# Neighbour sums by one float32 product in place of two float32r terms

## The chip, the cores and the metric

The kernel runs on one core of a Trainium2 chip. The metric is the device time of one execution in microseconds (us); lower is better. The engines are named as in the profile: PE is TensorE (matmuls), PEld its weight loads, DVE is VectorE, ACT is ScalarE, POOL is GpSimd and SP is SyncE, which only issues DMAs here.

## The reference

There are 4096 nodes with 512 features each, an adjacency matrix of 4096 x 4096 integers of 0 or 1 (a share of 0.0078 ones), and two layers.

```python
# layer 0
Ab = adj > 0
keep = Ab & (cumsum(Ab, axis=1) <= 64)            # the first 64 neighbours of each row
cnt = keep.sum(axis=1, keepdims=True)
nb_mean = (keep @ x) / maximum(cnt, 1.0)
xj = leaky_relu(nb_mean @ W_nb.T + b_nb)
xi = leaky_relu(x @ W_line.T + b_line)
x = layernorm(x + xi + where(cnt > 0, xj, 0))
# layer 1
Wh = x @ W + bW
e = (Wh @ a1 + b1)[:, None] + (Wh @ a2 + b2)[None, :]
e = where(e > 0, e, 0.2 * e)
e = where(adj > 0, e, -9e15)
x = layernorm(x + softmax(e, axis=1) @ Wh)
```

## The kernel before

The rows are cut into NB = 32 blocks of P = 128. The order of instructions on each engine is written by hand (`tc.manual_schedule()`): each engine executes its own in program order. Layer 0 computes y = x @ W_nb.T first, and then the neighbour sums keep @ y, which is the same as (keep @ x) @ W_nb.T.

**The maps.** A loop over g = 1 to NT - 1 = 15 (and a last call that finishes) calls `seven(g, last, codes)` for a pair of blocks. It computes x @ W_nb.T and x @ W_line.T for both with seven half products in place of eight, by sums and differences of operands (Winograd's form of Strassen's scheme). A product is two matmuls of 512 float32 columns (L512). PE adds into PSUM banks `bank_x`, `bank_y`, `bank_z` and `bank_w`; ACT copies between banks (L568, L578, L579), and DVE adds (L576, L594), forms the sums of x (L503 to L508) and transposes x in squares of 32 (L297). `y_terms` takes each block of y out of PSUM: ACT writes `y_hi`, y rounded to float32r (L427), and DVE writes `y_lo` = y - `y_hi` (L428). Blocks 26 to 29 have no room yet: they are kept whole and written to `y_d` in DRAM (L426); `room_again` takes back rooms that the maps used and loads these four blocks, and at step 2 of the sums they are split in two (L730, L731).

**The chunks of flags.** Between the steps of a round the kernel works on the adjacency matrix in chunks of 128 rows by CH = 2048 columns, two for each block, 64 in all. For one chunk: `load_adj` loads 1 MB by SP's queue into one of two buffers; `edge` (L171, ACT) makes flags of it; `scan_sums` (L189 to L194, DVE) counts along the row; `scan_codes` (L201 and L202, DVE) writes what remains after the limit of 64; `pack` (L219, ACT) makes bytes of it, and POOL's queue writes them to `code_d` in DRAM (L222). A variable `done` counts chunks. Rounds 3 to 15 take one chunk each, 13 in all; the other 51 lie in the next stage.

**The neighbour sums.** A loop over s = 0 to 127: block i = s // 4, and within it group g = s % 4 of KB = 8 tiles. `load_kt` loads the bytes of a block back with a transposing DMA, two blocks ahead; `make_kt` (L274, ACT) turns them into a tile of flags `kt` of 8 x 128 x 128, two steps ahead. PE then runs, for each of the 8 tiles j, one matmul against `y_hi` and one against `y_lo`, each with the flags as the stationary operand and 512 columns:

```python
for term in (y_hi, y_lo):
    nc.tensor.matmul(
        accs[i], kt[:, k // 2, k % 2, :], term[j],
```

This line is L757 in the profile. DVE and ACT finish the block before (bias, leaky ReLU, the block's own part, layer norm; `finish`), and `codes_step` spreads the remaining chunks at 58/32 of a chunk for each block.

**Layer 1** follows (L1221 and L908: Wh, again with seven products in place of eight; L1094: attention times Wh, four steps q in each of 16 pairs of blocks, 28 matmuls of 256 columns in each step). All its matmuls are float32.

Of the kernel before, what the change touches and what calls it, by code (L numbers as in the profile page):

```python
# [9 lines left out]
F32 = mybir.dt.float32  # L10
F32R = mybir.dt.float32r
# [4 lines left out]
ALU = mybir.AluOpType  # L16
# [4 lines left out]
P = 128  # L21
# [11 lines left out]
def two_layer_adj_gnn(  # L33
# [16 lines left out]
    nc = tc.nc  # L50
    N, C = x.shape
    NB = N // P
    NC = C // P
    NT = NB // 2
    CH = 2048
    NCH = N // CH
# [40 lines left out]
    own_d = [dram.tile([P, C], F32, name=f"own_d{b}") for b in range(NB)]  # L97
    y_d = dram.tile([P, 4, C], F32, name="y_d")

# [38 lines left out]
    with ExitStack() as l0:  # L138
        adj_p = l0.enter_context(tc.tile_pool(name="l0_adj", bufs=2))
        big = l0.enter_context(tc.tile_pool(name="l0_big", bufs=1))  # L140

        last = l0.enter_context(tc.tile_pool(name="l0_last", bufs=1, reuse_waits="tile"))
        ROOM = 6
        EDGE = NB - ROOM
        y_most = [big.tile([P, EDGE, C], F32R, name=name) for name in ("y_hi", "y_lo")]
        y_hi, y_lo = ({i: t[:, i, :] for i in range(EDGE)} for t in y_most)
        ident = big.tile([P, P], F32, name="ident")
# [6 lines left out]
        def load_adj(s, behind=None):  # L154
            if s < NB * NCH:
                b, h = divmod(s, NCH)
                a = adj_p.tile([P, CH], I32, name="a")
                if behind is not None:
                    behind.memset(a[:, 0:1].bitcast(F32), 0.0)
                nc.sync.dma_start(a, adj_blk(b)[:, ts(h, CH)])  # L160
                loaded[s] = a
# [103 lines left out]
        ktbs, kts, accs, owns, fin = {}, {}, {}, {}, {}  # L265
        y_again = []

        def make_kt(s):
            if s < NB * NS:
                b, g = divmod(s, NS)  # L270
                if s not in kts:
                    kts[s] = ktb_p.tile([P, KB // 2, 2, P], F32R, name="kt")
                bytes_ = ktbs[b].bitcast(U8)[:, ts(g, KB // 2), :]
                nc.scalar.activation(  # L274
                    kts[s], bytes_.rearrange("p t (i r) -> p t r i", r=2),
                    AF.Sigmoid, bias=steep[:, 1:2], scale=STEEP,
                )


        with ExitStack() as la:  # L280
            work = la.enter_context(tc.tile_pool(name="l0_work", bufs=2))
            wp = la.enter_context(tc.tile_pool(name="l0_w", bufs=1))

            AHEAD = 14
            bias_line = wp.tile([P, C], F32, name="bias_line")
            w_t = {}
            xrs, xbs, xts, pys, pls = {}, {}, {}, {}, {}
            lines, held = {}, []

# [105 lines left out]
            def fold_end():  # L395
                nc.vector.tensor_tensor(ca, ca, b12, ALU.add)
                nc.sync.dma_start(wa_d.rearrange("k (c p) -> p k c", p=P), wa)
# [20 lines left out]

            def y_terms(i, src):

                if EDGE <= i < NB - 2:
                    if not held:
                        held.extend((work.tile([P, C], F32, name="xb", bufs=1), room_lo[:, 5]))
                    t = held[i % 2]
                    nc.scalar.copy(t, src)
                    return lambda: nc.gpsimd.dma_start(y_d[:, i - EDGE, :], t)  # L426
                nc.scalar.copy(y_hi[i], src)  # L427
                return lambda: nc.vector.tensor_tensor(  # L428
                    y_lo[i], src, y_hi[i].bitcast(F32), ALU.subtract
                )  # L430

# [38 lines left out]

            room_hi = last.tile([P, ROOM, C], F32, name="hi")
            room_lo = last.tile([P, ROOM, C], F32, name="lo")

            def halves(t):
                return t.rearrange("p (k c) -> p k c", c=P)

            t1, t2, t4 = (room_hi[:, 2 * k : 2 * k + 2, :] for k in range(3))
            s1, s2, s4 = (
                halves(room_lo[:, k // 2, ts(k % 2, C // 2)]) for k in range(3)
            )  # L480
            w11, w21 = w_t["nb"][:, 0:2, :], w_t["nb"][:, 2:4, :]
# [5 lines left out]
            for k in range(2):  # L487
                x_low[2 * k] = halves(room_lo[:, 2 + k])

# [26 lines left out]

            y_low = [y_terms(i, pys[i]) for i in range(2)]
            turn_pair(1, 0)
# [11 lines left out]
            nc.scalar.copy(bank_z, bias_line)  # L530
            y_low[0]()
            tt(a21, a11, a21, ALU.subtract)
# [3 lines left out]
            bend(1)  # L536
            y_low[1]()
            tt(t4, w21, t2, ALU.subtract)
# [12 lines left out]
            line_tiles = [work.tile([P, C], F32, name="t", bufs=4) for _ in range(4)]  # L551
            line_tiles.append(room_lo[:, 4])

            def seven(g, last, codes):
# [9 lines left out]
                if old and new:  # L564
                    y_terms(2 * p, bank_y)()
                if new:
# [33 lines left out]
                if old and new:  # L600
                    y_terms(2 * p + 1, x_p)()
                if last:
                    room_again()
                    y_terms(2 * p, bank_y)()
                    y_terms(2 * p + 1, x_p)()
                if new:
# [11 lines left out]
            def make_first_kt():  # L618
                spare = adj_p.tile([P, CH], BF16, name="edge")
                kts[0] = spare.bitcast(F32R).rearrange("p (t r i) -> p t r i", r=2, i=P)  # L620

            def room_again():
                for y, name in ((y_hi, "hi"), (y_lo, "lo")):
                    t = last.tile([P, ROOM, C], F32R, name=name)
                    y_again.append(t[:, 0:4, :])
                    y.update((EDGE + n, t[:, n, :]) for n in range(ROOM))
                nc.sync.dma_start(y_again[1].bitcast(F32), y_d)

            idle = [lambda: None] * 4
            for g in range(1, NT):  # L630
                steps = idle
                q = done[0]
                if g == 1:
                    steps = [
                        lambda: None,
                        lambda: None,
                        lambda: nc.scalar.activation(few[:, 5:6], three, AF.Sigmoid),
                        lambda: fold_w(0),
                    ]
                elif g == 2:  # L640
                    steps = [
                        lambda: (fold_w(1), load_adj(0, nc.vector)),
                        lambda: fold_w(2),
                        lambda: None,
                        lambda: (fold_w(3), load_adj(1, nc.vector)),
                    ]
                else:
                    flags = lambda: (load_adj(q + 2), edge(q + 1))
                    codes = (lambda: pack(q - 1)) if g > 3 else (
                        lambda: (edge(0), fold_w(NC), fold_end())  # L650
                    )

                    steps = [
                        flags if g > 4 else codes,
                        lambda: scan_sums(q),
                        codes if g > 4 else flags,
                        lambda: scan_codes(q),
                    ]
                    if g == NT - 1:
                        load_own_x(NB - 1, nc.gpsimd)  # L660
                        scan_first = steps[1]
                        steps[1] = lambda: (scan_first(), load_first_kt())
                    done[0] += 1
                seven(g, False, steps)
# [6 lines left out]
        ktb_p = l0.enter_context(tc.tile_pool(name="l0_ktb", bufs=3, reuse_waits="tile"))  # L671
        RATE = 58 / 32
        start = done[0]

        def load_kt(b):
# [49 lines left out]
        for s in range(NB * NS):  # L725
            i, g = divmod(s, NS)
            if s == 2:
                for n in range(0, 4, 2):
                    hi, lo = (t[:, n : n + 2, :] for t in y_again)
                    nc.scalar.copy(hi, lo.bitcast(F32))  # L730
                    nc.vector.tensor_tensor(lo, lo.bitcast(F32), hi.bitcast(F32), ALU.subtract)  # L731
            make_kt(s + 2)
# [17 lines left out]
            kt = kts.pop(s)  # L750
            turns = list(range(KB))
            if s == NS - 1:
                turns = turns[:2] + turns[6:] + turns[2:6]
            for n, k in enumerate(turns):
                j = g * KB + k
                for term in (y_hi, y_lo):
                    nc.tensor.matmul(  # L757
                        accs[i], kt[:, k // 2, k % 2, :], term[j],
                        start=(g == n == 0 and term is y_hi),
                        stop=(g == NS - 1 and n == KB - 1 and term is y_lo),  # L760
                    )
            if g == 0:
                finish(i - 2, 4)
            finish(i - 1, g)
            codes_step(start + int((s + 1) * RATE / NS))
        finish(NB - 2, 4)
# [585 lines left out]
```

## Time and profile before

| | |
|---|---|
| time, median of 3 runs | 1550.87 us (1549.61 to 1551.31) |
| the profiled execution | 1549.75 us, its span 1548.0 us |
| granted TensorE clock | 0.999 |
| PE busy | 1537.9 us, 99% |
| DVE busy | 1265.5 us, 82% |
| ACT busy | 985.5 us, 64% |
| POOL busy | 269.5 us, 17% |
| HBM | 142.08 MB read, 43.13 MB written |

Times in the profile are microseconds unless marked ns. A busy time is the union of an engine's instructions; a matmul's record lasts until its last result is out, so records of consecutive matmuls overlap, and the time from the start of one to that of the next (its stride) is shorter than the record. The chain is the work that ended last, followed back from the last instruction.

### The profile page before, as it was taken

To read this page: it belongs to the slowest core of one execution; us is meant where nothing else is said; L and a number is where in the kernel's file an instruction comes from. 1 tells how busy PE (TensorE), PEld (TensorE's weight loads), DVE (VectorE), ACT (ScalarE), POOL (GpSimd) and SP (SyncE) were. 2 spreads that over 40 slices of the span, in tenths; PEclk is the share of its full clock that TensorE was granted. 3 is DMA by queue.
4 is the path that set the end of the run, shared out by engine and by line. 5 is a ranking of instruction groups with operands and counts; after the bars stand their busy time and mean duration, and the time that the engine had idled before them with its cause. 6 is when DMAs were issued, how large, how long until landed. Compare 5 with 4: busy or idle time off the path is not lost.

```text
span 1548.0 us, 19196 instructions
## 1 busy us (share of the span) xinstructions
PE 1537.9 (99%) x6592; PEld 1241.4 (80%) x6592; DVE 1265.5 (82%) x2349; ACT 985.5 (64%) x1190; POOL 269.5 (17%) x428
## 2 busy tenths in 40 slices
PE   9999999999999999999999999999999999999998
PEld 5444478888888888878888888888888888888887
DVE  6888759999999999378887888888888888888864
ACT  3666678888888887427685567555675556755520
POOL 4445322212222212120001101111011110111101
PEclk9999999999999999999999999999999999999999
DMA  7965598879888887653122212222122221222201
GB/s 196 249 208 185 192 251 265 251 244 256 259 257 256 238 263 193 152 135 104 47 58 55 51 32 69 66 58 51 32 69 67 57 52 33 68 67 57 52 4 55
DMA packets 178434, 203.28 MB, mean 131 GB/s; under 512 B 102224, under 2 KB 138832, under 8 KB 170016
## 3 DMA queue, kind: packets, MB, share of 16 engines
q1 hardware_dynamic: 150080, 131.78, 30.2%
q0 software_dynamic: 26544, 68.69, 16.9%
q10 hardware_dynamic: 1712, 1.59, 0.4%
q8 instruction: 52, 0.85, 0.2%
q14 instruction: 46, 0.38, 0.1%
HBM read 142.08 MB, written 43.13 MB: 120 GB/s over the span
## 4 chain that ended last, share of the span: by engine, by line
PE 98%; DMA 1%; DVE 1%; ACT 0%; ACTq 0%; issue 0%; POOLq 0%; DVEq 0%; SPq 0%
PE acc L1094 36%; PE acc L757 28%; PE pt L1094 14%; PE acc L512 11%; PE acc L908 5%; PE pt L757 2%; PE acc L1221 1%; DMA bias_line<-in_L_gnn_b_line_dram 0%; DMA a<-in_L_gnn_W_nb_dram 0%; DMA c<-in_x_dram 0%; PE acc L373 0%; PE acc L350 0%; DVE t L406 0%; DVE hi L519 0%; DVE hi L534 0%; ACTq L292 0%
## 5 line engine op out<-in xcount | busy, mean ns | idle before, releaser
L1094 PE MATMUL acc<-bt,s 128*128 128x256 f32 x1504 | 335.7, 379 | 0.0
L1094 PEld LDWEIGHTS acc<-bt,s 128*128 128x128 f32 x1504 | 285.8, 190 | 38.9
L757 PE MATMUL acc<-y_hi,kt 128*128 128x512 f32 x780 | 303.4, 389 | 0.0
L757 PE MATMUL acc<-y_lo,kt 128*128 128x512 f32 x780 | 303.4, 389 | 0.0
L979 ACT ACTIVATE w<-nat,few 128x1024 f32<-128x1024 uint8 x128 | 137.0, 1137 | 237.8 <-DVE a L1054 237.8
L1094 PE MATMUL acc<-bt,a 128*128 128x256 f32 x1056 | 239.0, 379 | 0.0
L1094 PE MATMUL pt<-bt,a 128*128 128x256 f32 x992 | 224.5, 379 | 0.0
L1094 PEld LDWEIGHTS acc<-bt,a 128*128 128x128 f32 x1056 | 200.6, 190 | 27.3
L1094 PEld LDWEIGHTS pt<-bt,a 128*128 128x128 f32 x992 | 188.5, 190 | 25.6
L1054 DVE STREAM_TRANSPOSE a<-w 128x1024 f32<-128x1024 f32 x128 | 153.2, 1226 | 61.5 <-ACT w L1035 51.0
L274 ACT ACTIVATE kt<-ktb,few 128x1024 fp32r<-128x1024 uint8 x124 | 142.7, 1152 | 87.4 <-PE acc L757 71.7
L127 POOL TENSOR_TENSOR rs<-ve,few 128x1 f32<-128x1 f32 x64 | 46.8, 731 | 811.0 <-DVE ve L125 791.1
L757 PEld LDWEIGHTS acc<-y_lo,kt 128*128 128x128 f32 x780 | 146.5, 188 | 30.5
L757 PEld LDWEIGHTS acc<-y_hi,kt 128*128 128x128 f32 x780 | 146.3, 188 | 30.4
L972 ACT ACTIVATE w<-w,st_n 128x1024 f32<-128x1024 f32 x128 | 149.3, 1233 | 16.1 <-DVE m L989 16.1
L1035 ACT ACTIVATE w<-w,nm 128x1024 f32<-128x1024 f32 x128 | 145.5, 1138 | 11.1 <-DVE nm L1026 11.1
L989 DVE CUSTOM_DVE_ANT_0 w<-e_n,w 128x1024 f32<-128x1024 f32 x128 | 149.5, 1221 | 1.3
L171 ACT ACTIVATE edge<-a,few 128x2048 bf16<-128x2048 int32 x64 | 136.3, 2130 | 6.0 <-DMA a<-in_adj_dram 6.0
L219 ACT CAST code<-left 128x2048 uint8<-128x2048 bf16 x64 | 121.1, 1892 | 0.0
L202 DVE TENSOR_TENSOR left<-edge,left 128x2048 bf16<-128x2048 bf16 x64 | 78.4, 1225 | 2.2
L190 DVE TENSOR_TENSOR_SCAN left<-few,ends,left 128x1024 bf16<-128x1024 f32 x32 | 75.2, 2351 | 1.1
L512 PE MATMUL acc<-hi,lo 128*128 128x512 f32 x160 | 73.8, 593 | 0.4 <-ACT acc L568 0.4
(236 smaller groups left out, 2048.6 us busy)
## 6 DMA issues: line engine op xcount, KB each, us to landing
a<-in_adj_dram SPq DMA_DIRECT2D x64, 1024.0 KB, 5.7
code_d<-code POOLq DMA_DIRECT2D x64, 256.0 KB, 3.8
nat<-code_d SPq DMA_DIRECT2D x248, 64.0 KB, 2.2
w<-x_d SPq DMA_DIRECT2D x128, 64.0 KB, 2.2
own<-in_x_dram SPq DMA_DIRECT2D x31, 256.0 KB, 3.1
own<-own_d POOLq DMA_DIRECT2D x31, 256.0 KB, 4.6
x_d<-own POOLq DMA_DIRECT2D x31, 256.0 KB, 4.4
out_dram<-c POOLq DMA_DIRECT2D x30, 256.0 KB, 2.8
```

Source lines behind the costliest of these rows:

```text
L171: nc.scalar.activation(edge_of[s], loaded.pop(s).rearrange("p (t q) -> p q t", q=2), AF.Sigmoid, bias=steep[:, 0:1], scale=STEEP, accum_ou ...
L202: nc.vector.tensor_tensor(left, e, left, ALU.mult)
L219: nc.scalar.copy(code.bitcast(U8).rearrange("p (t q) -> p q t", q=2), seen_of.pop(s))
L274: nc.scalar.activation(kts[s], bytes_.rearrange("p t (i r) -> p t r i", r=2), AF.Sigmoid, bias=steep[:, 1:2], scale=STEEP,)
L512: nc.tensor.matmul(bank, lhs[:, k, :], rhs[:, k, :], start=start and k == 0, stop=k == 1, skip_group_check=True,)
L757: nc.tensor.matmul(accs[i], kt[:, k // 2, k % 2, :], term[j], start=(g == n == 0 and term is y_hi), stop=(g == NS - 1 and n == KB - 1 and ...
L972: nc.scalar.activation(dst, src, AF.Prelu, bias=bias, scale=scale, alpha=0.2)
L979: nc.scalar.activation(wts[b][:, i, :], nats[b, i // 2].bitcast(U8)[:, i % 2, :], AF.Relu, bias=far, scale=-FAR,)
L989: nc.vector.tensor_tensor_reduce(w_i, e2_n, w_i, 1.0, -3e38, ALU.subtract, ALU.max, m4s[b][:, i : i + 1])
L1035: nc.scalar.activation(w_i, w_i, AF.Exp, bias=nms[b][:, i : i + 1], accum_out=z4s[g][:, r, i : i + 1])
L1054: nc.vector.transpose(a[:, r].rearrange("p s (i a) -> p i s a", a=SQ), wts[2 * g + r][:, :, ts(k, 8 * SQ)].rearrange("p i (s x) -> p i s x ...
L1094: nc.tensor.matmul(banks[g][n], lhs[:, j, :], bt[:, 4 * k + j, rhs, :], start=(k == 0 and j == 0 and n == mate[0]), stop=(k == NP - 1 and ...
```

## The change

y is kept whole, in float32: `y_all` holds all 32 blocks, `keep_y` is one copy by ACT, and the subtraction, the spill to `y_d`, `room_again` and the late splitting go. `kt` is float32, and each tile of flags is multiplied once by y (L734 of the changed kernel). The rooms of the maps become tiles of a pool of their own, `room_p`. Three more chunks of flags are placed in the maps, 16 in place of 13: the pairs of rounds 6 and 7, 9 and 10, 12 and 13 take three chunks each. The remaining 48 are spread evenly over 116 of the 128 steps of the sums.

```diff
-        y_most = [big.tile([P, EDGE, C], F32R, name=name) for name in ("y_hi", "y_lo")]
-        y_hi, y_lo = ({i: t[:, i, :] for i in range(EDGE)} for t in y_most)
+        y_all = big.tile([P, NB, C], F32, name="y")
...
-                    kts[s] = ktb_p.tile([P, KB // 2, 2, P], F32R, name="kt")
+                    kts[s] = ktb_p.tile([P, KB // 2, 2, P], F32, name="kt")
...
-            def y_terms(i, src):
-
-                if EDGE <= i < NB - 2:
-                    if not held:
-                        held.extend((work.tile([P, C], F32, name="xb", bufs=1), room_lo[:, 5]))
-                    t = held[i % 2]
-                    nc.scalar.copy(t, src)
-                    return lambda: nc.gpsimd.dma_start(y_d[:, i - EDGE, :], t)
-                nc.scalar.copy(y_hi[i], src)
-                return lambda: nc.vector.tensor_tensor(
-                    y_lo[i], src, y_hi[i].bitcast(F32), ALU.subtract
-                )
+            def keep_y(i, src):
+                nc.scalar.copy(y_all[:, i, :], src)
...
-                    flags = lambda: (load_adj(q + 2), edge(q + 1))
-                    codes = (lambda: pack(q - 1)) if g > 3 else (
-                        lambda: (edge(0), fold_w(NC), fold_end())
-                    )
-
-                    steps = [
-                        flags if g > 4 else codes,
-                        lambda: scan_sums(q),
-                        codes if g > 4 else flags,
-                        lambda: scan_codes(q),
-                    ]
+                    half = {6: 0, 7: 1, 9: 0, 10: 1, 12: 0, 13: 1}.get(g)
...
+                    elif half == 1:
+                        steps = [
+                            lambda: (pack(q - 1), scan_codes(q)),
+                            lambda: scan_sums(q + 1),
+                            lambda: flags(q + 1),
+                            lambda: (pack(q), scan_codes(q + 1)),
+                        ]
+                        done[0] += 1
+                    else:
+                        steps = [
+                            lambda: flags(q),
+                            lambda: scan_sums(q),
+                            lambda: pack(q - 1),
+                            lambda: scan_codes(q),
+                        ]
+                        if half == 0:
+                            steps[3] = lambda: (scan_codes(q), flags(q + 1), scan_sums(q + 1))
...
-            if s == 2:
-                for n in range(0, 4, 2):
-                    hi, lo = (t[:, n : n + 2, :] for t in y_again)
-                    nc.scalar.copy(hi, lo.bitcast(F32))
-                    nc.vector.tensor_tensor(lo, lo.bitcast(F32), hi.bitcast(F32), ALU.subtract)
...
-            for n, k in enumerate(turns):
+            for k in range(KB):
                 j = g * KB + k
-                for term in (y_hi, y_lo):
-                    nc.tensor.matmul(
-                        accs[i], kt[:, k // 2, k % 2, :], term[j],
-                        start=(g == n == 0 and term is y_hi),
-                        stop=(g == NS - 1 and n == KB - 1 and term is y_lo),
-                    )
+                nc.tensor.matmul(
+                    accs[i], kt[:, k // 2, k % 2, :], y_all[:, j, :],
+                    start=(j == 0), stop=(j == NB - 1),
+                )
...
-            codes_step(start + int((s + 1) * RATE / NS))
+            codes_step(start + (s + 1) * AFTER // (NS * (NB - 3)))
```

More of the change, by code (lines that the diff above doesn't have):

```diff
@@ L97, in two_layer_adj_gnn @@
     own_d = [dram.tile([P, C], F32, name=f"own_d{b}") for b in range(NB)]
-    y_d = dram.tile([P, 4, C], F32, name="y_d")
     x1_d = [dram.tile([N // 4, C], F32, name=f"x1_d{k}") for k in range(4)]
@@ L140, in two_layer_adj_gnn @@
         big = l0.enter_context(tc.tile_pool(name="l0_big", bufs=1))
-        last = l0.enter_context(tc.tile_pool(name="l0_last", bufs=1, reuse_waits="tile"))
-        ROOM = 6
-        EDGE = NB - ROOM
-        y_most = [big.tile([P, EDGE, C], F32R, name=name) for name in ("y_hi", "y_lo")]
-        y_hi, y_lo = ({i: t[:, i, :] for i in range(EDGE)} for t in y_most)
+        y_all = big.tile([P, NB, C], F32, name="y")
         ident = big.tile([P, P], F32, name="ident")
@@ L265, in two_layer_adj_gnn @@
         ktbs, kts, accs, owns, fin = {}, {}, {}, {}, {}
-        y_again = []
         def make_kt(s):
@@ L282, in two_layer_adj_gnn @@
             wp = la.enter_context(tc.tile_pool(name="l0_w", bufs=1))
+            room_p = la.enter_context(tc.tile_pool(name="l0_room", bufs=1))
             AHEAD = 14
@@ L287, in two_layer_adj_gnn @@
             xrs, xbs, xts, pys, pls = {}, {}, {}, {}, {}
-            lines, held = {}, []
+            lines = {}
             def load_squares(dst, src, queues):
@@ L465, in two_layer_adj_gnn @@
             wide = [pls[0]]
[L471 to L479, printed above, removed]
-            )
+            t1, t2, t4 = (room_p.tile([P, 2, C], F32, name=f"t{k}") for k in (1, 2, 4))
+            s1, s2, s4 = (room_p.tile([P, 2, P], F32, name=f"s{k}") for k in (1, 2, 4))
             w11, w21 = w_t["nb"][:, 0:2, :], w_t["nb"][:, 2:4, :]
@@ L487, in two_layer_adj_gnn @@
             for k in range(2):
-                x_low[2 * k] = halves(room_lo[:, 2 + k])
+                x_low[2 * k] = room_p.tile([P, NC, P], F32, name=f"x_low{k}")
             def top(g):
@@ L515, in product @@
                     )
-            y_low = [y_terms(i, pys[i]) for i in range(2)]
+            for i in range(2):
+                keep_y(i, pys[i])
             turn_pair(1, 0)
@@ L530, in two_layer_adj_gnn @@
             nc.scalar.copy(bank_z, bias_line)
-            y_low[0]()
             tt(a21, a11, a21, ALU.subtract)
@@ L536, in two_layer_adj_gnn @@
             bend(1)
-            y_low[1]()
             tt(t4, w21, t2, ALU.subtract)
@@ L551, in two_layer_adj_gnn @@
             line_tiles = [work.tile([P, C], F32, name="t", bufs=4) for _ in range(4)]
-            line_tiles.append(room_lo[:, 4])
+            line_tiles.append(room_p.tile([P, C], F32, name="line"))
             def seven(g, last, codes):
@@ L564, in seven @@
                 if old and new:
-                    y_terms(2 * p, bank_y)()
+                    keep_y(2 * p, bank_y)
                 if new:
@@ L600, in seven @@
                 if old and new:
-                    y_terms(2 * p + 1, x_p)()
+                    keep_y(2 * p + 1, x_p)
                 if last:
-                    room_again()
-                    y_terms(2 * p, bank_y)()
-                    y_terms(2 * p + 1, x_p)()
+                    keep_y(2 * p, bank_y)
+                    keep_y(2 * p + 1, x_p)
                 if new:
@@ L619, in make_first_kt, with flags @@
                 spare = adj_p.tile([P, CH], BF16, name="edge")
[L620 to L627, printed above, removed]
+                kts[0] = spare.bitcast(F32).rearrange("p (t r i) -> p t r i", r=2, i=P)
+            def flags(q):
+                load_adj(q + 2)
+                edge(q + 1)
             idle = [lambda: None] * 4
@@ L647, in two_layer_adj_gnn @@
                 else:
-                    flags = lambda: (load_adj(q + 2), edge(q + 1))
-                    codes = (lambda: pack(q - 1)) if g > 3 else (
-                        lambda: (edge(0), fold_w(NC), fold_end())
-                    )
-                    steps = [
-                        flags if g > 4 else codes,
-                        lambda: scan_sums(q),
-                        codes if g > 4 else flags,
-                        lambda: scan_codes(q),
-                    ]
+                    half = {6: 0, 7: 1, 9: 0, 10: 1, 12: 0, 13: 1}.get(g)
+                    if g < 5:
+                        codes = (lambda: pack(q - 1)) if g > 3 else (
+                            lambda: (edge(0), fold_w(NC), fold_end())
+                        )
+                        steps = [
+                            codes, lambda: scan_sums(q), lambda: flags(q), lambda: scan_codes(q)
+                        ]
[8 more added lines that the diff above has]
+                    else:
+                        steps = [
+                            lambda: flags(q),
+                            lambda: scan_sums(q),
+                            lambda: pack(q - 1),
+                            lambda: scan_codes(q),
+                        ]
+                        if half == 0:
+                            steps[3] = lambda: (scan_codes(q), flags(q + 1), scan_sums(q + 1))
                     if g == NT - 1:
@@ L671, in two_layer_adj_gnn @@
         ktb_p = l0.enter_context(tc.tile_pool(name="l0_ktb", bufs=3, reuse_waits="tile"))
-        RATE = 58 / 32
         start = done[0]
+        AFTER = NB * NCH + 1 - start
         def load_kt(b):
@@ L750, in two_layer_adj_gnn @@
             kt = kts.pop(s)
-            turns = list(range(KB))
-            if s == NS - 1:
-                turns = turns[:2] + turns[6:] + turns[2:6]
-            for n, k in enumerate(turns):
+            for k in range(KB):
                 j = g * KB + k
-                for term in (y_hi, y_lo):
-                    nc.tensor.matmul(
-                        accs[i], kt[:, k // 2, k % 2, :], term[j],
-                        start=(g == n == 0 and term is y_hi),
-                        stop=(g == NS - 1 and n == KB - 1 and term is y_lo),
-                    )
+                nc.tensor.matmul(
+                    accs[i], kt[:, k // 2, k % 2, :], y_all[:, j, :],
+                    start=(j == 0), stop=(j == NB - 1),
+                )
             if g == 0:
```

## The prediction

> **What bounds the kernel now.** I read the page first: which engine is busy, and what the chain that ended last is made of.
>
> ```profile
> span 1548.0 us, 19196 instructions
> PE 1537.9 (99%) x6592; PEld 1241.4 (80%) x6592; DVE 1265.5 (82%) x2349; ACT 985.5 (64%) x1190; POOL 269.5 (17%) x428
> PE 98%; DMA 1%; DVE 1%; ACT 0%; ACTq 0%; issue 0%; POOLq 0%; DVEq 0%; SPq 0%
> ```
>
> TensorE (PE) is busy and carries 98% of the chain, so time comes from what is put on or taken off PE; work on the others is hidden until it makes PE wait. Next, the chain in order of time (start, us, what), which says how long each PE stage lasts.
>
> ```profile
> 26.76 177.09 PE acc L512 x412
> 203.85 29.31 PE pt L757 x128
> 233.16 435.20 PE acc L757 x1920
> 668.36 10.30 PE acc L1221 x24
> ```
>
> L512 are the maps, L757 the neighbour sums, L1221 the start of layer 1. They abut: maps end at 203.85, and the sums run from there to 668.36 without a gap, 464.51 us in 2048 records. Then the two lines themselves (count, duration in ns as minimum/median/maximum, first and last start).
>
> ```profile
> L757 PE MATMUL acc<-y_hi,kt x780: 389/389/389, 233.0 to 665.0; 128*128 128x512 f32 x195
> L757 PE MATMUL acc<-y_lo,kt x780: 389/389/389, 233.2 to 665.3; 128*128 128x512 f32 x195
> L757 PEld LDWEIGHTS acc<-y_lo,kt x780: 187/188/188, 233.0 to 665.0; 128*128 128x128 f32 x195
> L512 PE MATMUL acc<-hi,lo x160: 592/592/697, 24.5 to 203.3; 128*128 128x512 f32 x160
> L512 PEld LDWEIGHTS acc<-hi,lo x160: 186/190/190, 24.0 to 202.8; 128*128 128x128 f32 x160
> ```
>
> The type column says f32 for both, but L757's operands are float32r and L512's plain float32, and they differ twice. Durations overlap, so a record's price is its stride in the chain: 464.51 / 2048 = 226.8 ns for float32r, 177.09 / 412 = 429.8 ns for float32 of the same 512 columns. And the count: the code issues 2 x 32 x 32 = 2048 float32r matmuls and the trace has 2048 records, one each. In the maps it issues 15 rounds x 7 products x 2 = 210 matmuls, and the groups of L512 add up to 160 + 120 + 100 + 20 + 20 = 420: two records for each float32 matmul. L1094 agrees: 4 x 16 x 28 = 1792 matmuls in code, 1504 + 1056 + 992 + 32 = 3584 records.
>
> **The sums (main term).** Removed: 2048 float32r matmuls, 464.5 us. Added: 32 blocks x 32 tiles = 1024 matmuls of float32 flags by float32 y, 512 columns. No row shows flags as a float32 operand, but the L512 rows have the same shape, type and one weight load per record, so I price them by these: 1024 x 2 x 429.8 ns = 880.2 us. One product costs 859.7 ns where its two terms cost 453.6. Difference: 880.2 - 464.5 = +415.7 us, all on the path. Bounds from the other float32 rows: L1221, 10.30 / 24 = 429.2 ns, gives 879.0 us; L1094's stride for 256 columns (8.63 us for 40 records, 215.75 ns), doubled, 883.7 us. So +414.5 to +419.2.
>
> Two rules were weighed. The cheapest record of 512 columns strides 226.8 ns, and a float32 one nearly twice that. The Trainium skill, "TensorE: Matmul & The Clock Gate", section "Back-to-back issue gap", has about 131 ns per matmul of 512 columns as sustained spacing in a stream of loads and matmuls; with the four passes that "FP8 and Floating Point Precision", section "TensorE Precision Notes", counts for true FP32, the sums would take 1024 x 4 x 131 ns, an estimated 537 us from these pages, and the change would cost only some 72 us. No row comes near 131, so the measurement decides. Secondly, the weight loads take 188 ns in float32r and 190 in float32, under strides of 226.8 and 429.8, so nothing of a difference there is on the path. The first page's section "Weight-path perf modes — Fast Weight Load (FWL) and DoubleRow" says that fast loads are off for FP32 operands, which would speak against the change; these rows show 2 ns of it.
>
> **Other engines in the longer stage.** Per step of 8 tiles PE will take 8 x 859.7 = 6.88 us instead of 3.63. In the 435.50 us from 233.0, DVE is busy 379.06 and ACT 339.94. Fewer chunks are left there (48 scans in place of 51), and the rest spreads over 116 of 128 steps, so both fall to under half load. The nearest deadline is the last: block 31's second chunk is done at about step 115, its transposing load is issued at step 116, and its first tile of flags is made at step 122, some 41 us later, against 3.8 us for the write and a few for the load. The tile of flags costs ACT 1.15 us per 6.88 us step, made two steps ahead. I take 0.
>
> **Three more chunks in the maps.** Rounds 6/7, 9/10 and 12/13 carry three chunks per pair instead of two. Cover now, in one round (us; busy and count of PE, PEld, DVE, ACT, POOL; clock; DMA share; GB/s):
>
> ```profile
> 99.00:111.00 12.00, 12.00 (x30) 5.30 (x29) 10.15 (x15) 7.97 (x11) 6.00 (x11) 1.00 0.66 227
> ```
>
> A round is 28 records x 429.8 = 12.04 us. By the timeline a chunk takes 5.04 us of DVE (106.64 to 109.82, and 100.98 to 102.84) and about 4.2 of ACT (2.18 + 0.22 for the edge, 1.89 for the codes). The change also takes away two subtractions y_lo = y - y_hi per round, 128x512, 0.6 us each by stride (102.84 to 104.03 for two); ACT's copy of y stays. DVE per pair: 2 x 10.15 - 2.4 + 5.04 = 22.9 of 24.1 us; ACT: 2 x 7.97 + 4.2 = 20.1. It fits, tightly, so the order counts. In a first round an extra scan (3.15 us) follows the codes; laid on the times above, round 99.0 would end its DVE work at 106.0, and the next would do a transpose, the codes and a transpose before L576's addition, done at 109.9 instead of 106.7. PE overwrites that bank from 111.2: 1.3 us to spare. L594's addition is then done at 114.2, and PE writes into its source bank at 116.4: 2.2 us to spare. On ACT, each first round ends with an extra edge (2.2 us), with the copy of y, and the next round's copies, queued behind it; its load was issued some 8 us earlier and lands in 5.7, and the bank copy behind it is wanted by PE only at the round's last product. On SP only these loads stand in line (3 MB more); POOL issues three more code writes of 0.58 us, beside 6.0 busy of 12. I take 0; a few us of waits per pair would give up to +8 in all; no gain is possible, as L512 strides show no wait.
>
> **The edges.** At 26.3 PE waits 0.43 us for ACT's copy at L568, behind a DVE chain with one early y_lo subtraction (22.48, 0.6 us). It goes: -0.4 (0 at least). Dropped beside hidden work: four spills of y through DRAM (256 KB each), their 1 MB load back, and the late splitting at step 2 (two ACT copies and two DVE subtractions). In the trace PE enters L757 without a wait, so these earn 0. After the sums nothing changes: layer 1 waits for the last block alone.
>
> **Sum.** Profiled execution: 1549.75 (span 1548.0 and 1.75 around it) + 415.7 + 0 - 0.4 = 1965.05. The median of the runs, 1550.87, is 1.12 above the profiled one: 1966.2, say 1966.
>
> **Rivals.**
> *The sums get faster.* Mechanism: a float32 matmul against flags is one record rather than two. For it: the change halves the matmul instructions, and 1024 x 429.8 = 440.1 us is 24.4 less than now: 1550.9 - 24.4 - 0.4 = 1526. If float32 streamed as float32r does, 232.2 us of PE would lie under DVE's 398 us (379.1 + 19.3) and the time near 1485. It decides from below 453.6 ns per product. Against: all 2002 float32 matmuls of L512 and L1094, two records each, whatever their operands hold. This is also the case in which the change isn't what its types say. 3%.
> *The maps wait.* If DVE's order costs what the three chunks add in full, 3 x 5.04 = 15 us: 1981. For it: margins of 1.3 us, and DVE at 22.9 of 24.1; against: removed subtractions, and a DVE that now idles some 2 us per round waiting for PE. 5%.
> *The sums wait as well.* Transposing loads or flags late at the end of the stage: a step or two of 6.88 us, up to 1980. Against it, load under half. 1%.
> *Forecast*, PE-bound with two records per product: 91%.
>
> **Range and chances.** Base 1549.6 to 1551.3, sums +414.5 to +419.2, maps 0 to +8, edge -0.4 to 0: 1963.7 to 1978.5. The ends don't fall together; 1962 to 1975 leaves out the first rival, the full price of the second and part of the third, under 2 in 10. About 0.2%, 3 us, is what a measurement of this kernel tells from no change. Faster 0.03, same 0, slower 0.97.
>
> **What would show it.** Right: the product's line (L734 after) has 2048 records at a stride near 430 ns and spans about 880 us; L512's successor keeps 12.04 us per round; DVE and ACT each under half busy in the sums; PE still 98% of the chain or more. Wrong: 1024 records, or a stride that is not 430 ns; PE waits in the maps for DVE's L576 or L594 successors in rounds 7, 10 and 13; a gap before the first neighbour product.

## The result, and the profile after

| | before | after |
|---|---|---|
| time, median | 1550.47 us (1549.61 to 1551.31, 4 runs) | 1966.68 us (1966.53 to 1967.15, 4 runs) |
| ratio | | 1.2685, 95% interval 1.2663 to 1.2707 |
| span of the profiled execution | 1548.0 us | 1965.0 us |
| maps (start, length) | 26.76, 177.09 us | 27.34, 177.09 us |
| neighbour sums | 464.5 us | 879.2 us |
| from the end of the sums to the end | 879.6 us | 881.4 us |

The changed kernel is slower by 27%; 1966 was predicted. The lines that answer to those shown of before: first the page after (span, busy times, the chain by engine).

```profile
span 1965.0 us, 19170 instructions
PE 1952.8 (99%) x6592; PEld 1245.5 (63%) x6592; DVE 1251.7 (64%) x2319; ACT 986.6 (50%) x1188; POOL 272.0 (14%) x424
PE 98%; DVE 1%; DMA 1%; issue 0%; ACT 0%; ACTq 0%; POOLq 0%; DVEq 0%; POOL 0%; SPq 0%
```

PE has as many records as before, 6592, though the program has 1024 matmul instructions fewer, and it is busy 415 us longer. DVE and ACT do nearly what they did (DVE 14 us less); their shares fall because the span grew. The chain in order of time (start, us, what) gives the stages; L489 are the maps of the changed kernel, L734 its neighbour sums:

```profile
27.34 177.08 PE acc L489 x412
204.43 55.20 PE pt L734 x128
259.63 824.01 PE acc L734 x1920
```

The product's line alone (count, ns as minimum/median/maximum, first and last start):

```profile
L734 PE MATMUL acc<-y,kt x1920: 592/592/593, 259.5 to 1083.0; 128*128 128x512 f32 x192
L734 PEld LDWEIGHTS acc<-y,kt x1920: 190/190/190, 259.0 to 1082.6; 128*128 128x128 f32 x192
```

2048 records for 1024 products, 592 ns long like those of the maps, where the float32r terms had 389; 879.21 us / 2048 = 429.3 ns each. The stage in one row (columns: length, then busy time and count of PE, PEld, DVE, ACT, POOL, then granted clock, DMA share, GB/s):

```profile
204.43:1083.64 879.21, 879.20 (x2048) 389.03 (x2048) 381.38 (x609) 352.02 (x303) 107.23 (x146) 1.00 0.44 120
```

PE is busy in all of it at full clock, DVE in 43% and ACT in 40%. The spans differ by 417.0 us: 414.7 in the sums, 0 in the length of the maps, 0.58 in their start, 1.72 after the sums.

### The profile page after: what moved, and what is told of

It is laid out like the page before. It is cut to its first block, busy times and chain, and to the rows that moved or that the text cites. A ratio compares the mean times of both kernels' runs of the same rounds, so it can differ in the third digit from the quotient of the medians.

```text
span 1965.0 us, 19170 instructions
## 1 busy us (share of the span) xinstructions
PE 1952.8 (99%) x6592; PEld 1245.5 (63%) x6592; DVE 1251.7 (64%) x2319; ACT 986.6 (50%) x1188; POOL 272.0 (14%) x424
## 4 chain that ended last, share of the span: by engine, by line
PE 98%; DVE 1%; DMA 1%; issue 0%; ACT 0%; ACTq 0%; POOLq 0%; DVEq 0%; POOL 0%; SPq 0%
PE acc L734 42%; PE acc L1070 28%; PE pt L1070 11%; PE acc L489 9%; PE acc L884 4%; PE pt L734 3%; DMA bias_line<-in_L_gnn_b_line_dram 0%; DMA a<-in_L_gnn_W_nb_dram 0%; DMA c<-in_x_dram 0%; PE acc L1197 0%; PE acc L368 0%; PE acc L345 0%; DVE c L816 0%; DVE w L704 0%; DVE w L816 0%
## 5 line engine op out<-in xcount | busy, mean ns | idle before, releaser
L734 PE MATMUL acc<-y,kt 128*128 128x512 f32 x1920 | 824.2, 592 | 0.0
L734 PEld LDWEIGHTS acc<-y,kt 128*128 128x128 f32 x1920 | 364.8, 190 | 459.2 <-issue 459.2
L268 ACT ACTIVATE kt<-ktb,few 128x1024 f32<-128x1024 uint8 x124 | 142.8, 1151 | 508.3 <-PE acc L734 389.9
L126 POOL TENSOR_TENSOR rs<-ve,few 128x1 f32<-128x1 f32 x64 | 51.8, 809 | 890.9 <-DVE ve L124 890.7
L692 DVE SCALAR_TENSOR_TENSOR own<-t,e,own 128x512 f32<-128x512 f32 x31 | 23.3, 752 | 215.7 <-ACT t L679 215.7
L184 DVE TENSOR_TENSOR left<-edge 128x1024 bf16<-128x1024 bf16 x64 | 43.9, 685 | 123.2 <-ACT code L214 122.8
L217 POOL DMA_DIRECT2D code_d<-code x64 | 35.4, 553 | 532.5 <-ACT code L214 371.1
L686 DVE SCALAR_TENSOR_TENSOR t<-acc,rcnt,c 128x512 f32<-128x512 f32 x29 | 21.8, 750 | 89.7 <-PE acc L734 89.7
```

What stands on the lines that cost most here:

```text
L268: nc.scalar.activation(kts[s], bytes_.rearrange("p t (i r) -> p t r i", r=2), AF.Sigmoid, bias=steep[:, 1:2], scale=STEEP,)
L734: nc.tensor.matmul(accs[i], kt[:, k // 2, k % 2, :], y_all[:, j, :], start=(j == 0), stop=(j == NB - 1),)
```

## The experiments

The theory: the number of TensorE records and the stride of each set the time; a float32 product is two records of 429 ns, a float32r term one of 227. The rivals: the other half of the change (the chunks' place) has a share in it; the price belongs to the stage and not to the product; or another engine sets the pace.

**The float32 product alone** (e1_f32_13_chunks, 4 runs). The edit takes the three chunks out of the maps again and leaves the rest of the change as it is:

```diff
-                    half = {6: 0, 7: 1, 9: 0, 10: 1, 12: 0, 13: 1}.get(g)
+                    half = None
```

> One part of the change alone: the float32 product, with 13 chunks of flags in the maps as before (the other 51 in the sums). Theory (TensorE's records set the time, two per float32 matmul, and the place of the chunks is hidden): sums 879 us in 2048 records, maps 177.1 us, 1966.5 us, the same as the changed kernel within 2 us. Rival (the chunks' place matters): over 3 us away, lower if three more chunks cost the maps time that no wait shows, higher if 51 chunks no longer fit beside the sums.

Measured: 1966.58 us against 1550.14 before, ratio 1.2683 (1.2665 to 1.27), sums again 2048 records in 879.2 us:

```profile
205.26 55.20 PE pt L734 x128
260.46 824.01 PE acc L734 x1920
```

The three chunks' place changes nothing that can be measured beside the product. This kernel also keeps y whole in one tile and drops the subtractions, so its time alone does not part the product from these. The chain does: 414.7 of the 416.4 us lie in the sums.

**The 16 chunks alone** (e2_f32r_16_chunks, 11 runs), y still in two float32r terms. The edit puts the changed kernel's `half` branches in place of `steps` in the kernel before:

```diff
-                    flags = lambda: (load_adj(q + 2), edge(q + 1))
...
+                    half = {6: 0, 7: 1, 9: 0, 10: 1, 12: 0, 13: 1}.get(g)
...
```

> The other part alone: 16 chunks in the maps, y still in two float32r terms. Sums as before, 464.5 us. Maps: with the two subtractions per round still there, a pair of rounds with three chunks has 2 x 10.15 + 5.04 = 25.3 us of VectorE work in 24.1 us. Theory (VectorE's order is what the removed subtractions made room for): PE waits about 1 us in each of the three pairs, 1551.5 to 1556 us. Rival (there was room anyway, since what is late is caught up in the rounds between): 1550.5 us, no waits of PE in the maps.

Measured: 1554.05 us, 3.9 more than before, ratio 1.0024 (1.0015 to 1.0033). The chain of this kernel in the maps (start, us, what):

```profile
59.73 28.34 PE acc L512 x66
88.16 0.69 DVE acc L594
...
100.09 0.58 DVE t L576
100.72 24.32 PE acc L512 x56
125.13 0.70 DVE acc L594
...
137.07 0.58 DVE t L576
137.69 24.32 PE acc L512 x56
```

Where before and after have one unbroken run of L512, here the chain leaves PE in each pair of rounds, goes through DVE's queue, and comes back at L576's addition, the one whose source bank PE overwrites. The period is 137.69 - 100.72 = 36.97 us, for three rounds of 12.04 us, 36.12: 0.85 us lost per pair. Maps: 207.56 - 27.70 = 179.86 us, 2.77 more than before; most of what is left of the difference in span (1551.8 against 1548.0) is a start of the maps that came 0.94 later.

From the start of L594 to the end of L576 this kernel takes 12.51 us (88.16 to 100.67). In the changed kernel their successors are L570 and L552, and the same stretch takes 11.46 us (87.79 to 99.25). Its end, with the product that overwrites the bank behind it (start, us, what; in brackets the idle time before and what ended it):

```profile
98.60 0.65 DVE L552 TENSOR_TENSOR t<-t,acc 128x512 f32<-128x512 f32 x1
99.30 0.43 PEld L489 LDWEIGHTS acc<-t,x_low 128*128 128x128 f32 x2 [0.43 <-DVE t L552]
99.54 1.88 PE L489 MATMUL acc<-t,x_low 128*128 128x512 f32 x4
```

The weight load did wait for L552, as it does in all three pairs, but the matmul starts on time, 1.72 us after the product before it. Where PE was held up, at 100.72, load and matmul start together, 0.05 us after the addition; so L552 could have ended some 0.24 us later at no cost. The 1.05 us by which the stretch is longer here, less these 0.24, are about the 0.85 lost per pair. The theory holds: removing two subtractions of 0.6 us made the room for the chunks, and only just. The run e7 below agrees: it is the changed kernel with the subtractions back in, and its maps take the same 179.86 us.

**Half of the products** (e3_half_f32, 4 runs), 13 chunks:

```diff
+                if j < NB // 2:
+                    for term in (y_hi, y_lo):
+                        nc.tensor.matmul(accs[i], flags_j, term[:, j, :], ...)
+                else:
+                    nc.tensor.matmul(accs[i], flags_j.bitcast(F32), y_whole[:, j - NB // 2, :], ...)
```

> Half of the change: tiles 0 to 15 as two float32r terms, tiles 16 to 31 whole in float32, 13 chunks in the maps. Theory (each float32 product costs 859 ns where two terms cost 454, one by one): 512 x 859 + 1024 x 226.8 = 672 us of sums, 207 us over the kernel before, 1758 us. Rival (the price is of the stage, by switching of modes or another engine): not halfway, over 10 us off.

Measured: 1760.21 us, ratio 1.1352 (1.1336 to 1.1367). Its chain over two blocks:

```profile
254.28 13.73 PE acc L749 x32
268.01 7.27 PE acc L744 x32
275.28 13.73 PE acc L749 x32
289.01 7.27 PE acc L744 x32
```

L749 are the 16 float32 products of a block, 32 records in 13.73 us; L744 the 32 float32r terms of the other 16 tiles, 7.27 us. The types alternate within a block, and each keeps its stride, 429.1 and 227.2 ns; the sums take 672.3 us, where 672 were expected. The price belongs to the product; it is not one of the stage.

**One float32r term** (e4_one_f32r_term, 2 runs):

```diff
-        y_all = big.tile([P, NB, C], F32, name="y")
+        y_all = big.tile([P, NB, C], F32R, name="y")
...
-                    kts[s] = ktb_p.tile([P, KB // 2, 2, P], F32, name="kt")
+                    kts[s] = ktb_p.tile([P, KB // 2, 2, P], F32R, name="kt")
```

> The changed kernel with y and the flags in float32r, one product per tile: what float32r rounds off y is left out. Theory: 1024 records, one per product, 232 us of TensorE, so that the sums stop being bound by it; VectorE's 381 us and ScalarE's 352 us of the stage set the pace, with waits of PE on the tile of flags: sums 390 to 430 us, 1478 to 1518 us. Rival (a product is two records for these tiles, or PE still sets the pace): sums 464 us, 1551 us, or 232 us, 1320 us.

Measured: 1526.0 us (1522.9 and 1529.09), 24.7 below the kernel before measured beside it (1550.69), ratio 0.9843 (0.9795 to 0.9892). The forecast of the stage held, that of the time did not. The stage, columns as above:

```profile
204.30:624.60 420.30, 287.27 (x1024) 208.26 (x1024) 369.30 (x595) 340.80 (x302) 93.97 (x142) 0.89 0.88 244
```

1024 records for the same number of products: float32r is one record where float32 is two, so the count comes from the type. The sums take 420 us with PE busy 287, at a granted clock of 0.89. PE no longer sets the pace: it waited 128.8 us for tiles of flags from ACT. DVE and the DMA engines are both busy 88%, and which of the two holds ACT up was not separated. What was missed lies behind the stage: PE waited another 14.1 us there for the first transpose of layer 1. The chain runs there through loads one behind another: own rows (3.26 and 4.07 us), W of layer 1 (5.66) and its x (5.46). The lower time is paid for in precision: this kernel leaves out what float32r rounds off y.

**Two bfloat16 terms** (e5_bf16_terms, 5 runs), 13 chunks: is the 226.8 ns of float32r the floor for a record?

```diff
+        y_hi, y_lo = (big.tile([P, NB, C], BF16, name=n) for n in ("y_hi", "y_lo"))
...
+                    kts[s] = ktb_p.tile([P, KB // 2, 2, P], BF16, name="kt")
```

> Flags in bfloat16 and y in two bfloat16 terms (8 and 8 bits in place of float32r's two terms), 13 chunks in the maps. Theory (one record per product for any type but float32; 226.8 ns is float32r's own stride and 512 columns stream in half of a float32 record, 214.9 ns): sums about 441 us, 23 us less than before, 1527 us. Rival A (226.8 ns is set by loading the flags for each matmul, whatever the type): 464 us, 1550. Rival B (VectorE, with 398 us of work in that stage, sets the pace at times): waits of PE on the tile of flags, 1530 to 1545.

Measured: 1538.57 us, ratio 0.9923 (0.991 to 0.9937): 0.8% faster than before, and 11.6 us slower than the theory said. Who waited in the stage (engine and line, for whom: us in total, times, longest):

```profile
PE acc L736 <- ACT kt L268: 6.9, 3, 5.5
PEld L736 <- ACT kt L268: 9.6, 6, 6.0
ACT edge L166 <- DMA a<-in_adj_dram: 11.5, 3, 7.1
```

The stage runs from 205.47 to about 657.4, 452 us, where 2048 x 215.8 is 442. Rival B describes the waits: PE and its weight loads waited for tiles of flags, and DVE is busy 393.3 us of the 449.6 from 205.4. But the cause is not DVE alone. The longest wait, before 578.96, ends a chain that runs on DVE almost without a break until 554, then on ACT, and then through a load of the matrix, which took 8.29 us from 567.25 and held ACT up for 7.1.

**The same with 14 and 16 chunks in the maps** (e8_bf16_14_chunks, e7_bf16_16_chunks, 4 runs each), `half` with one pair of rounds and with three:

> The same with 14 chunks in the maps (one pair of rounds with three). Theory: maps +0.9 us, sums 446 to 450 us, 1534 to 1537 us, between the runs with 13 and 16 chunks. Rival: 1539 us, as with 13.

> Two bfloat16 terms again, now with the 16 chunks of the change in the maps. Sums of the bfloat16 run with 51 chunks beside them: 452 us, where 2048 records x 215.8 = 442, and waits of PE for the tile of flags. Theory (VectorE and ScalarE have too little room there, 393 and 358 us of 450): with 48 chunks the waits go, sums 442 to 445 us, maps +2.8 us as with float32r terms, 1531 to 1534 us. Rival (a late load of the matrix is the cause, whatever the number of chunks): sums 452 us again, 1541 us.

Measured, with 14: 1535.86 us, ratio 0.9909 (0.9895 to 0.9922); with 16: 1531.04 us, ratio 0.988 (0.9866 to 0.9893). The chain and the loads of flags of the run with 16:

```profile
206.36 27.80 PE pt L736 x128
234.16 414.20 PE acc L736 x1919
...
L736 PEld LDWEIGHTS <-kt x2032: 97/98/98, 209.6 to 648.0; 128*128 128x128 bf16 x185
```

414.20 / 1919 = 215.8 ns per record, 442.0 us of sums, and PE never waits for a tile of flags (only its first weight load does, 0.8 us, as in the kernel before). With 14 chunks the sums took 445.7 us, with 13 about 452. So the chunks in the maps, which are worth nothing beside a float32 product, are worth 7.5 us here (1538.57 to 1531.04; the kernel before, measured beside each, differed by 0.4), although they cost the maps the waits seen above. Fewer chunks in the sums mean less work for DVE and ACT and fewer loads of the matrix there; the runs do not part these, but a load that is late whatever the number of chunks is ruled out. This is the fastest kernel of the study with two terms, 18.7 us below the kernel before; what bfloat16 terms cost in accuracy was not measured.

**y in two tiles** (e6_y_in_two_tiles, 5 runs): what are the 1.72 us after the sums?

```diff
-        y_all = big.tile([P, NB, C], F32, name="y")
+        y_first = big.tile([P, NB - 6, C], F32, name="y")
+        y_last = big.tile([P, 6, C], F32, name="y_last")
```

The line of layer 1's first transposes in the changed kernel, how long DVE sat idle before it and until what ended, and who waited for it (L1197 is the start of layer 1 on PE):

```profile
L816 DVE STREAM_TRANSPOSE w<-w x3: 669/670/711, 1083.7 to 1084.9; 128x512 f32<-128x512 f32 x3
...
  PE acc L734: 14.2, 1
...
  PEld acc L1197: 1.6, 1
  PE acc L1197: 0.8, 1
```

> The changed kernel with y_all cut into two tiles, 26 blocks and 6 blocks, nothing else. After the sums of the changed kernel PE waits 0.80 us for a transpose and 0.71 us for a copy, and the first transposes of layer 1 waited 14.2 us for the neighbour products, while before they waited 1.5 us; they write where the first blocks of y lay. Theory (the room of y as one tile comes free only with the last product, in two tiles 12 records earlier): these waits go, 1965.0 us. Rival (the waits come from the load of the last rows or from noise): 1966.7 us, waits as they were.

Measured: 1964.99 us (1964.34 to 1968.43), 1.7 us less than the changed kernel. The ranges of the two overlap, and the kernel before, measured beside each, differs by 0.7, so the time alone would not settle it; the trace of this kernel does, in its transposes and its chain:

```profile
L821 DVE STREAM_TRANSPOSE w<-w x3: 669/669/711, 1081.6 to 1082.9; 128x512 f32<-128x512 f32 x3
1079.88 6.87 PE acc L739 x16
1086.75 10.30 PE acc L1202 x24
```

The transposes start 5.15 us before the end of the sums, which is 12 records of 429.3 ns; in the changed kernel they start after it (1083.7 against 1083.64). The sums (L739) and layer 1 (L1202) abut, and no wait of PE is left there; from 1086.75 to the end at 1966.3 it takes 879.55 us, as before (879.64). A buffer of y that lies under layer 1's tiles came free only with the last product. The profiled execution itself took 1968.43 us, because its sums began 3.1 us later than those of the changed kernel: the load of W_nb landed after 6.13 us in place of 4.57, and the first eight matmuls behind it took 1.97 us in place of 1.09.

## Why the prediction was right

Point by point:

- **The price of a product.** 859.7 ns predicted, 2 x 429.3 = 858.6 measured; over the stage +415.7 us predicted, +414.7 measured. The count of two records per float32 matmul, inferred from the maps and from L1094, held for flags of 0 and 1.
- **The rules.** No record of 512 columns came near 131 ns: the lowest stride of any run is 215.8 (bfloat16). With the 131 ns the prediction weighed four passes for a float32 product; 858.6 ns are four times 214.7, so the times speak against the 131 and not against the four, though the trace shows two records and no passes. The second rule, which the Trainium skill states in "TensorE: Matmul & The Clock Gate", section "Weight-path perf modes — Fast Weight Load (FWL) and DoubleRow", is that fast loads are off for FP32 operands. The runs agree as far as they go: the load of a tile takes 98 ns in bfloat16, 188 in float32r and 190 in float32. If the 98 ns are such a fast load, which no run here shows, float32r had none to lose, and the change cost none.
- **The other engines in the stage.** Taken at 0, and right: PE never waits for a tile of flags. Only its first weight load does, 0.8 us, as in the kernel before.
- **Three more chunks.** Taken at 0, and right: 177.09 us, and L552 and L570 in front of PE in all pairs. DVE's work per pair came out near what was reckoned, 22.54 us against 22.9 (10.62 and 11.93 in the two rounds from 86.5). But the room left before PE was worked out as 1.3 us and was about 0.24. Two things were missed. PE writes into that bank from 110.98 in the kernel before, by its own record, not from 111.2. And each first round of a pair ends a block, whose counts take DVE five more operations (L204 to L208, 0.88 us). So the 0 held by little, and in part by luck; the waits of e2 show how near it was.
- **The edges.** This step failed. -0.4 us was predicted for the early subtraction; the maps began 0.58 us later, still with a wait of 0.42 us. The subtraction is gone from the chain, and from the landing of the last load of x to this product it is 6.71 us in place of 7.36. But that load ended at 20.62 instead of 19.40 us. Landings differ between executions by more than the term: W_nb took 4.18 us before, 4.57 after and 6.13 in e6, and a term of 0.4 us at the start could not have been told from that.
- **After the sums.** "Nothing changes" was wrong by 1.72 us. Before, `y_hi` and `y_lo` ended with tile 25, and the last six tiles lay in rooms of their own, so that layer 1's transposes could start 12 records before the end (at 665.5, of 668.36); one tile of y for all blocks took that away. The sums were put 1.0 us too high, the two misses at the ends are worth 2.7 us the other way: 1.7 together, in a difference of 417.0.
- **The median.** 1966.2 was worked out and 1966.68 measured, and that it is so close is in part luck. The profiled execution was put at 1965.05 and took 1967.15 us; the median was put 1.12 above it and came out 0.47 below.
- **The rivals.** None occurred. The first would have needed one record per product, which the runs show for float32r (e4) and bfloat16 (e7), not for float32.

## What to carry to other kernels

Price a matmul by records times stride from rows of the same type and shape, and count the records against the code: instructions halved here while the records stayed and each took 1.9 times as long. Here two terms in a type of one record each beat one product in float32 (454 or 432 ns against 859), and among such types the stride still differs (227 against 216 ns). Work moved off a crowded stage is worth something only where that stage's bound is close: the same three chunks were worth nothing under float32 and 7.5 us under bfloat16, and cost 3.9 us under float32r, where PE set the pace of the sums and the maps had no room for them.

## What had not been expected of the hardware

float32r strides 226.8 ns for 512 columns where bfloat16 strides 215.8, with loads of flags of 188 and 98 ns. That the slower load is the cause of the 11 ns was only argued from these two numbers: a mix of bfloat16 flags with float32r y was not run. And with PE waiting often (e4) the granted clock in the stage was 0.89, and 0.97 in the 100 us of e5 that hold its waits, where the stages with PE busy throughout show 1.00; what ties the two was not tried.
